# A selective-scan layer and a linear-attention layer in one kernel: the recurrence re-laid as 32 channels by 4 states on the partitions

## The chip, the cores and the metric

The kernel runs on one core of a Trainium2 chip. The metric is the device time of one execution in microseconds (us); less is better. The core has five instruction queues that run side by side, each strictly in its written order: PE (matrix products; PEld is its loading of weights), DVE (vector work, the only engine used here that scans), ACT (functions of one input), POOL (vector work without access to PSUM) and SP, which issues the transfers.

## The reference, cut to what matters

`x` has shape (4, 512, 64, 64): four batches, 512 channels, 4096 positions. Two residual layers follow each other, each fed by a group norm. All data is f32.

```python
# layer 0, on tokens (L = 4096) in four chunks of 128 channels
xn = layer_norm(group_norm(x));  chunk -> 128 channels
xi, z = split(xn_chunk @ in_proj_w.T)            # 256 + 256
xc = silu(causal_conv(xi, 4 taps) + conv_b)      # 256 channels
dt, B, C = split(xc @ x_proj_w.T, 8, 16, 16)
dt = softplus(dt @ dt_proj_w.T + dt_proj_b);  A = -exp(A_log)
h[t] = exp(dt[t] * A) * h[t-1] + dt[t] * xc[t] * B[t]     # 256 channels x 16 states
y[t] = sum over states of h[t] * C[t]
y = (y + xc * D) * silu(z);  chunk_out = y @ out_proj_w.T + skip * xn_chunk
x1 = x + layer_norm(all chunks) @ proj_w.T + proj_b
# layer 1, attention without softmax, 8 heads of 64, on g = group_norm(x1)
q, k = relu(g @ w_q.T + b_q), relu(g @ w_k.T + b_k);  v = g @ w_v.T + b_v
kq = k^T q per head, summed over tokens;  attn = (v @ kq) / (column sums of kq)
out = x1 + attn @ w_out.T + b_out
```

## The kernel before

The positions are cut into 8 tiles of T = 512 for each batch. The unit of work is a **step**: one chunk (c = 0 to 3) of one tile (t) of one batch (b); there are 4 x 8 x 4 = 128 steps. Channels lie on the 128 partitions, so the 256 inner channels are two **halves** (index e), and time runs along the free dimension.

A step has these parts, and the names are those that the profile prints:

- `front` prepares a step while the one before it runs. PE computes `pc` (convolution and input projection folded, 4 matmuls a half) and `pz` (1 a half); ACT takes them out of PSUM (L332, L338; the **front evacuations**), applies silu to both (L297, with a table load before and after). PE computes `pd` (dt, B and C); ACT copies `dtr` and `parts` (L351, L355); L358 on DVE and L362 to L364 on POOL split C into three bf16 parts; the B rows go to DRAM (`b_rows`, L353). PE computes `pt`; five ACT instructions (L374, L375, L377) and then L381, L382 (DVE) and the logarithm L385 form the softplus. The **dt tail** on POOL ends it: `lw` (L387), `dt` (L388), `dtx` = dt * xc (L389), three instructions on 128 x 1024.
- `recurrence` goes through the 16 states. For each: `bx` = dtx * B on POOL (L403; B broadcast over the partitions by a transfer, `b_all`, L398, two states each); `c_all` on PE (L405, C broadcast over the partitions by a bf16 matmul, in the one buffer of the pool `ps_c`); for each half the decay `dA` = exp(A * dt) on ACT (L411, two PSUM buffers) and the scan `h` on DVE (L412), whose last column POOL keeps in `st` (L416); the product `ch` = h * c_all on DVE (L418); and on PE `y` += identity x `ch` (L423), which sums the states in PSUM, one bank a half.
- `gated` closes the step before, within the first state of the new one: the **D-add** on DVE (L431, one a half, reads `y`), the **gate product** on POOL (L434), `po` on PE (L437), and the **ym update** on DVE (L438).

A f32 matmul stands in the trace as two `MATMUL` **pieces**; so the 4096 `y` matmuls are 8192 there.

Three generators are interleaved with the recurrence by `behind()`, called 16 times a step: the next step's `front`; `late` (the next tile's normalisation with L208, L220 to L241; for the last tile the layer norm of `ym`, L223, and the projection `pp` into the residual, L267 to L276); and `rest` (statistics of the next batch and attention of the one before). Attention goes twice over the tiles: first `pq` (L466), the bias add (L472), relu (L475) and `pk` into `kq` (L480, L488); then, with the weights folded into `m3`, the output product `pr` (L546) of the normalised `x1` (L208) with the residual add (L552). It runs within the steps of the next batch, so in batches 1 to 3, and for the last batch after all steps.

All is written for a scheduler that takes these instructions by priority and its own estimates of time and writes out the five queues, and the semaphores; so the order in a queue may differ from that of the text. Every buffer is one of a named pool; a transfer that fills it waits on SP until its last reader is done. The lines of the recurrence that the prediction follows:

```python
c_all = ps_c.tile([P, T], F32, tag="c", name=f"c_all_{nm}_{s}")          # ps_c: bufs=1
nc.tensor.matmul(c_all, sel[:, s : s + 1].to_broadcast([NP, P]), f["parts"], start=True, stop=True)
...
nc.vector.tensor_tensor(ch, h, bc(c_all, NH), ALU.mult)
if s == 0:
    before()                                                             # gated() of the step before
for e in range(NH):
    nc.tensor.matmul(ys[e], ident, ch[:, e, :], start=(s == 0), stop=(s == NST - 1))
behind()
```

Of the kernel before, what the change touches and what calls it, by code (L numbers as in the profile page):

```python
# [14 lines left out]
P = 128  # L15
# [9 lines left out]
def kernel(  # L25
# [33 lines left out]
    NB = 2  # L59
# [16 lines left out]
    def load(src, name):  # L76
        xt = wk.tile([P, NC, T], F32, tag="x", name=name, bufs=4)
        nc.sync.dma_start(xt, src)
        return xt
# [21 lines left out]
    sel = const.tile([NP, NST], BF16, tag="sel", name="sel")  # L101
    for i in range(3):
        r = slice(i * LANE, (i + 1) * LANE)
        nc.vector.tensor_copy(sel[r, :], ident[r, i * LANE : i * LANE + NST])
# [20 lines left out]
    w_x = wk.tile([P, DI], F32, tag="bx", name="w_x", bufs=2)  # L125
    nc.scalar.dma_start(w_x, in_w[:, 0:DI])
    conv_bc = wk.tile([P, NTAP, DI], F32, tag="ch", name="conv_bc", bufs=2)
# [29 lines left out]
    bqk = const.tile([P, 2 * C], F32, tag="bqk", name="bqk")  # L157
    nc.scalar.dma_start(bqk, b_qkv[0 : 2 * C].partition_broadcast(P))
    bv = column(b_qkv[2 * C : 3 * C], NC, "bv")
    bo = column(b_out, NC, "bo")  # L160


    nc.scalar.activation(a_sb, a_sb, AF.Exp)
    nc.vector.tensor_scalar(a_sb, a_sb, -1.0, None, ALU.mult)
# [16 lines left out]
    def stats_end(stats, name):  # L181
# [20 lines left out]
        nc.vector.scalar_tensor_tensor(off, gm, -1.0, gr, ALU.mult, ALU.mult)  # L202
        return gr, off

    def group_norm(dst, xt, norm):
        gr, off = norm
# [39 lines left out]
    def normed(xn, prev, b, t, norm):  # L246

        xt = load_x(b, t, "f")
# [5 lines left out]
        body = xn[:, :, NTAP - 1 : NTAP - 1 + T]  # L254
        group_norm(body, xt, norm)
# [52 lines left out]
    def front_tiles(nm):  # L308
        return {
            n: wk.tile([rows_, *shape], dt_, tag=n, name=f"{n}_{nm}")  # L310
            for n, rows_, shape, dt_ in (
                ("xz", P, (2, NH, T), F32),
                ("dt", P, (NH, T), F32),
                ("dtx", P, (NH, T), F32),
# [4 lines left out]
    def front(f, xn, c, nm):  # L319

        xz, dt, dtx, parts = (f[n] for n in ("xz", "dt", "dtx", "parts"))
# [35 lines left out]
        rest = w[0:NP, 0, :]  # L357
        nc.vector.tensor_tensor(rest, pd[0:NP, :], parts, ALU.subtract)  # L358
        yield
        mid = wk.tile([NP, T], BF16, tag="mid", name=f"mid_{nm}", bufs=1)  # L360
        r1, r2 = slice(LANE, 2 * LANE), slice(2 * LANE, 3 * LANE)
        nc.gpsimd.tensor_copy(parts[r1, :], rest[r1, :])  # L362
        nc.gpsimd.tensor_copy(mid[r2, :], rest[r2, :])
        nc.gpsimd.tensor_tensor(parts[r2, :], rest[r2, :], mid[r2, :], ALU.subtract)  # L364
# [24 lines left out]
        nc.gpsimd.tensor_tensor(dtx, dt, xc, ALU.mult)  # L389
        yield  # L390

    def recurrence(f, st, c, first, nm, before, behind):


        b_all = []
        for s in range(0, NST, NB):
            got = wk.tile([P, NB, T], F32, tag="b_all", name=f"b_all_{nm}_{s}", bufs=4)
            nc.sync.dma_start(got, f["b_rows"][s : s + NB, :].partition_broadcast(P))  # L398
            b_all.append(got)
        ys = []  # L400
        for s in range(NST):
            bx = wk.tile([P, NH, T], F32, tag="bx", name=f"bx_{nm}_{s}", bufs=2)
            nc.gpsimd.tensor_tensor(bx, f["dtx"], bc(b_all[s // NB][:, s % NB, :], NH), ALU.mult)  # L403
            c_all = ps_c.tile([P, T], F32, tag="c", name=f"c_all_{nm}_{s}")
            nc.tensor.matmul(  # L405
                c_all, sel[:, s : s + 1].to_broadcast([NP, P]), f["parts"], start=True, stop=True
            )
            h = wk.tile([P, NH, T], F32, tag="h", name=f"h_{nm}_{s}", bufs=2)
            for e in range(NH):
                dA = ps_d.tile([P, T], F32, tag="dA", name=f"dA_{nm}_{s}_{e}")  # L410
                nc.scalar.activation(dA, f["dt"][:, e, :], AF.Exp, scale=a_sb[:, e, s : s + 1])  # L411
                nc.vector.tensor_tensor_scan(  # L412
# [9 lines left out]
            for e in range(NH):  # L422
                nc.tensor.matmul(ys[e], ident, ch[:, e, :], start=(s == 0), stop=(s == NST - 1))  # L423
# [276 lines left out]
```

## Time and profile before

| what | value |
|---|---|
| median of 3 runs (lowest to highest) | 11519.98 us (11518.61 to 11539.81) |
| the profiled execution: its time, its span | 11542.73 us, 11541.0 us |
| busy: PE, DVE, POOL, ACT | 81%, 75%, 57%, 45% of the span |
| DVE busy, in us | 8695.3 |
| mean granted clock of PE | 0.928 |
| 185 to 2866 us (32 steps, batch 0) | 83.8 us a step |
| 2866 to 5649 us (32 steps, batch 1) | 87.0 us a step |
| 5649 to 8414 us (32 steps, batch 2) | 86.4 us a step |
| 8414 to 11009 us (31 steps, batch 3) | 83.7 us a step |
| 11009 to 11541 us (after the last gate product) | PE busy 439 of 532 us |
| moved by transfers | 793.56 MB, 19.7% of the 16 DMA engines' time |
| `b_all`: 1024 transfers of 512 KB, issue to landing | 3.6 us |
| loads and stores of 1024 KB tiles, issue to landing | 3.8 to 6.8 us |

A row of the costliest groups reads: line, engine, operation, output<-inputs, sizes, count | busy us, mean ns of one | the engine's idle time before these, and what ended most of it. Busy time is a union: pieces of matmuls overlap, so their busy time by count is less than the mean of one. The steps are cut at the starts of the 128 gate products (L434), the first at 185.1 us, the last at 11008.9. A waiting row reads: who waited <- for whom: us in total, times, longest. Shares are averages over the whole span; a step's time comes from which queue holds up which within it.

### The profile page before, as it was taken

Reading aid. Unit: us, or ns where it says so; the run is one execution under the profiler, and the core shown is the slowest. Engines: PE = TensorE matmul, PEld = TensorE weight load, DVE = VectorE, ACT = ScalarE, POOL = GpSimd, SP = SyncE. Lnnn points to the kernel's source line nnn. Section 1 sums busy time; section 2 is a strip of 40 time slices with the busy share of each in tenths; the row PEclk is TensorE's granted clock in tenths of the full one; section 3 lists DMA queues with packets and bytes.
Section 4 is the critical chain, followed back from the end, with each engine's and each line's share of the span. In section 5 each row is a group of like instructions: output and inputs, shape, how many; then the busy total and the mean of one; then the engine's idle time right before and its main releaser. Section 6 shows DMA issues by size and latency. Waiting matters only on the chain.

```text
span 11541.0 us, 69580 instructions
## 1 busy us (share of the span) xinstructions
PE 9309.0 (81%) x20832; PEld 3741.0 (32%) x20832; DVE 8695.3 (75%) x8177; ACT 5230.3 (45%) x7460; POOL 6599.1 (57%) x5045
## 2 busy tenths in 40 slices
PE   5777777777788888888788888888888888888878
PEld 2222222222333333333333333333333333333333
DVE  6777777787777777787877777777777887878831
ACT  3444444444444544444444444444444545444421
POOL 4666666566565565565566565566565665656600
PEclk8999898988899998999999999999999999999999
DMA  4111111121111111122311111122211111112201
GB/s 138 61 63 54 60 61 64 59 89 63 47 69 64 63 64 66 59 84 83 101 62 66 54 64 64 62 72 85 84 66 64 66 70 63 67 65 84 89 24 66
DMA packets 244443, 793.56 MB, mean 69 GB/s; under 512 B 27224, under 2 KB 27744, under 8 KB 231776
## 3 DMA queue, kind: packets, MB, share of 16 engines
q1 hardware_dynamic: 237184, 784.42, 19.7%
q10 hardware_dynamic: 6880, 4.70, 0.1%
q8 instruction: 163, 2.67, 0.1%
q14 instruction: 216, 1.77, 0.0%
HBM read 717.73 MB, written 71.30 MB: 68 GB/s over the span
## 4 chain that ended last, share of the span: by engine, by line
PE 36%; DVE 34%; POOL 15%; ACT 8%; issue 7%; DMA 0%; DVEq 0%; ACTq 0%; POOLq 0%; SPq 0%
DVE h L412 20%; PE y L423 14%; DVE ch L418 10%; PE pc L326 8%; POOL bx L403 7%; PE pq L466 4%; PE po L437 3%; POOL dt L388 2%; POOL dtx L389 2%; POOL lw L387 2%; POOL xz L434 2%; PE pz L334 2%; PE c_all L405 2%; ACT L297 1%; ACT xz L297 1%
## 5 line engine op out<-in xcount | busy, mean ns | idle before, releaser
L423 PE MATMUL y<-ch,ident 128*128 128x512 f32 x8192 | 4492.7, 676 | 1754.9 <-DVE ch L418 1753.3
L412 DVE TENSOR_TENSOR_SCAN h<-dA,st,bx 128x512 f32<-128x512 f32 x3584 | 4414.9, 1269 | 569.8 <-ACT dA L411 201.2
L403 POOL TENSOR_TENSOR bx<-dtx,b_all 128x1024 f32<-128x1024 f32 x2048 | 4819.0, 2353 | 0.7 <-POOL st L416 0.6
L411 ACT ACTIVATE dA<-dt,a_sb 128x512 f32<-128x512 f32 x4096 | 2815.2, 691 | 3793.0 <-DVE h L412 3778.0
L418 DVE TENSOR_TENSOR ch<-h,c_all 128x1024 f32<-128x1024 f32 x2048 | 2470.4, 1206 | 954.4 <-PE c_all L405 945.6
L423 PEld LDWEIGHTS y<-ch,ident 128*128 128x128 f32 x8192 | 1559.6, 205 | 4322.9 <-DVE ch L418 3063.7
L416 POOL COPY st<-h 128x2 f32<-128x2 f32 x2048 | 380.2, 186 | 4055.2 <-DVE h L412 4007.6
L466 PE MATMUL pq<-w_qk,xa 128*128 128x512 f32 x2048 | 982.6, 608 | 8.6 <-ACT xa L208 4.0
L326 PE MATMUL pc<-xn,w_cv 128*128 128x512 f32 x2048 | 971.8, 599 | 4.2 <-ACT xn L241 4.2
L405 PE MATMUL c_all<-parts,sel 96*128 96x512 bf16 x2048 | 825.3, 403 | 0.0
L332 ACT ACTIVATE xz<-pc,cb 128x512 f32<-128x512 f32 x256 | 175.9, 687 | 1411.9 <-PE pc L326 1411.7
L412 DVE TENSOR_TENSOR_SCAN h<-dA,bx 128x512 f32<-128x512 f32 x512 | 599.3, 1208 | 104.5 <-POOL bx L403 49.7
L466 PEld LDWEIGHTS pq<-w_qk,xa 128*128 128x128 f32 x2048 | 394.5, 196 | 470.9 <-issue 420.9
L326 PEld LDWEIGHTS pc<-xn,w_cv 128*128 128x128 f32 x2048 | 394.9, 193 | 465.1 <-issue 448.6
L267 PE MATMUL pp<-ym,w_pr 128*128 128x512 f32 x1024 | 491.4, 604 | 13.5 <-DVE ym L243 13.5
L546 PE MATMUL pr<-gn,m 128*128 128x512 f32 x1024 | 482.6, 602 | 12.9 <-ACT gn L208 9.6
L437 PE MATMUL po<-xz,w_op 128*128 128x512 f32 x512 | 315.3, 746 | 148.8 <-POOL xz L434 148.5
L472 DVE TENSOR_TENSOR qk<-pq,bqk 128x512 f32<-128x512 f32 x256 | 174.3, 681 | 298.8 <-PE pq L466 298.8
L405 PEld LDWEIGHTS <-sel 96*128 96x128 bf16 x2048 | 215.6, 105 | 558.3 <-issue 536.3
L387 POOL TENSOR_TENSOR lw<-lw,dtx 128x1024 f32<-128x1024 f32 x128 | 301.6, 2356 | 135.0 <-ACT lw L385 135.0
L438 DVE SCALAR_TENSOR_TENSOR ym<-xn,sk,po 128x512 f32<-128x512 f32 x128 | 95.7, 747 | 325.1 <-PE po L437 325.1
L346 PE MATMUL pd<-xz,w_xp 128*120 128x512 f32 x512 | 271.9, 654 | 77.0 <-ACT xz L297 77.0
(125 smaller groups left out, 7353.8 us busy)
## 6 DMA issues: line engine op xcount, KB each, us to landing
b_all<-b_rows SPq DMA_DIRECT2D x1024, 512.0 KB, 3.6
xs<-in_x_dram SPq DMA_DIRECT2D x32, 1024.0 KB, 6.3
xf<-in_x_dram SPq DMA_DIRECT2D x32, 1024.0 KB, 6.7
xr<-in_x_dram SPq DMA_DIRECT2D x32, 1024.0 KB, 5.7
x<-xr SPq DMA_DIRECT2D x32, 1024.0 KB, 3.8
xa<-x SPq DMA_DIRECT2D x32, 1024.0 KB, 5.3
xb<-x SPq DMA_DIRECT2D x32, 1024.0 KB, 5.1
out_dram<-xb SPq DMA_DIRECT2D x32, 1024.0 KB, 4.2
```

What stands on the lines that cost most here:

```text
L267: nc.tensor.matmul(pp, w_pr[:, c, o * P : (o + 1) * P], ym[:, c, :], start=(c == 0), stop=(c == NC - 1),)
L326: nc.tensor.matmul(pc, w_cv[:, k, e * P : (e + 1) * P], xn[:, c, k : k + T], start=(k == 0), stop=(k == NTAP - 1),)
L387: nc.gpsimd.tensor_tensor(w, w, q, ALU.subtract)
L403: nc.gpsimd.tensor_tensor(bx, f["dtx"], bc(b_all[s // NB][:, s % NB, :], NH), ALU.mult)
L405: nc.tensor.matmul(c_all, sel[:, s : s + 1].to_broadcast([NP, P]), f["parts"], start=True, stop=True)
L411: nc.scalar.activation(dA, f["dt"][:, e, :], AF.Exp, scale=a_sb[:, e, s : s + 1])
L412: nc.vector.tensor_tensor_scan(h[:, e, :], dA, bx[:, e, :], 0.0 if first else st[:, c, s, e : e + 1], ALU.mult, ALU.add,)
L418: nc.vector.tensor_tensor(ch, h, bc(c_all, NH), ALU.mult)
L423: nc.tensor.matmul(ys[e], ident, ch[:, e, :], start=(s == 0), stop=(s == NST - 1))
L437: nc.tensor.matmul(po, w_op[:, e, :], sz[:, e, :], start=(e == 0), stop=(e == NH - 1))
L466: nc.tensor.matmul(pq, gn[:, c, u * P : (u + 1) * P], w_qk[:, c, j * C : (j + 1) * C], start=(c == 0), stop=(c == NC - 1),)
L546: nc.tensor.matmul(pp, m3[:, m, o * P : (o + 1) * P], gn[:, m, :], start=(m == 0), stop=(m == NC - 1),)
```

## The change

The recurrence is laid out anew. A tile holds 32 channels by 4 states on its 128 partitions (partition = state index k in the group x 32 + channel), so a half of 128 channels is four blocks j, and the 16 states are four groups q. The recurrence goes through 8 groups (half e, group q), each with two **pairs** of blocks; a pair is one `bx`, two `dA`, two scans, one `st` copy and one product, of the same shapes as a state had before. The product is written over `bx` (three buffers, held until `y` has read it). One `c_all` serves a group, and the next group's is written ahead of this group's `y` in the text. `y` is summed by a 128 x 32 matrix `fold` (four stacked identities) into 32 of the 128 partitions. `dt` and `dtx`, one buffer now, go to DRAM (`d_rows`) after the dt tail and come back spread to the new layout (`spread`, eight transfers of 256 KB a half); `b_all` becomes four transfers of 64 KB a group. In attention the q/k bias enters through a bf16 matmul of three parts, relu reads PSUM, the second group norm is folded into `m3` (with an identity for the residual) and `ob`, and outputs leave by quarters of a tile. The input tile of a normalisation is loaded in place.

```diff
+        nc.vector.tensor_copy(
+            sel[r].rearrange("p q k i -> p (q k) i"),
+            ident[r, i * LANE : i * LANE + NST].unsqueeze(2).to_broadcast([LANE, NST, BLK]),
+        )
...
+    fold = const.tile([P, BLK], F32, tag="fold", name="fold")
+    for k in range(KS):
+        r = slice(k * BLK, (k + 1) * BLK)
+        nc.vector.tensor_copy(fold[r, :], ident[r, r])
...
-        xt = load_x(b, t, "f")
+        body = xn[:, :, NTAP - 1 : NTAP - 1 + T]
+        nc.sync.dma_start(body, cols(x, b)[:, :, t * T : (t + 1) * T])
...
-        xz, dt, dtx, parts = (f[n] for n in ("xz", "dt", "dtx", "parts"))
+        xz, parts = f["xz"], f["parts"]
+        both = wk.tile([P, 2, NH, T], F32, tag="dt", name=f"dt_{nm}", bufs=1)
+        dt, dtx = both[:, 0], both[:, 1]
...
         nc.gpsimd.tensor_tensor(dtx, dt, xc, ALU.mult)
-        yield
+
+        f["d_rows"] = []
+        for v in range(2):
+            d_rows = dram.tile([P, NH, T], F32, tag=f"d_rows{v}", name=f"d_rows{v}_{nm}")
+            nc.sync.dma_start(d_rows, both[:, v])
+            f["d_rows"].append(d_rows)
+        yield
+        spread(f, 0, nm)
+        yield
+
+    def spread(f, e, nm):
+        d = wk.tile([P, 2, NJ, T], F32, tag="d_all", name=f"d_all_{nm}_{e}")
+        for v in range(2):
+            src = f["d_rows"][v].rearrange("(j i) e t -> i e j t", i=BLK)[:, e]
+            for k in range(KS):
+                nc.sync.dma_start(d[k * BLK : (k + 1) * BLK, v], src)
+        f["d_all", e] = d
...
+        groups = [(e, q) for e in range(NH) for q in range(NQ)]
+        b_all = {g: b_row(*g) for g in groups[:NQ]}
+        c_all = c_row(*groups[0])
         ys = []
...
+        for n, (e, q) in enumerate(groups):
+            if n == 1:
+                spread(f, 1, nm)
+            if n == NQ - 1:
+                b_all.update({g: b_row(*g) for g in groups[NQ:]})
+            d = f["d_all", e]
+            chs = []
+            for jj in range(JJ):
+                k2 = f"{nm}_{e}_{q}_{jj}"
+                js = slice(jj * 2, jj * 2 + 2)
+                bx = wk.tile([P, 2, T], F32, tag="bx", name=f"bx_{k2}", bufs=3)
+                nc.gpsimd.tensor_tensor(bx, d[:, 1, js, :], bc(b_all[e, q], 2), ALU.mult)
+                h = wk.tile([P, 2, T], F32, tag="h", name=f"h_{k2}", bufs=2)
+                for i in range(2):
+                    j = jj * 2 + i
+                    dA = ps_d.tile([P, T], F32, tag="dA", name=f"dA_{k2}_{i}")
+                    nc.scalar.activation(dA, d[:, 0, j, :], AF.Exp, scale=a_t[:, e, j, q : q + 1])
+                    nc.vector.tensor_tensor_scan(
+                        h[:, i, :], dA, bx[:, i, :],
+                        0.0 if first else st[:, c, e, q, j : j + 1], ALU.mult, ALU.add,
+                    )
+                nc.gpsimd.tensor_copy(st[:, c, e, q, js], h[:, :, T - 1])
+
+                nc.vector.tensor_tensor(bx, h, bc(c_all, 2), ALU.mult)
+                chs.append(bx)
+                if n == 0 and jj == 0:
+                    before()
+                if jj < JJ - 1:
+                    behind()
+            if n + 1 < len(groups):
+                c_all = c_row(*groups[n + 1])
+            if q == 0:
+                ys.append(ps_y.tile([P, T], F32, tag="y", name=f"y_{nm}_{e}"))
+            for jj in range(JJ):
+                for i in range(2):
+                    r = slice((jj * 2 + i) * BLK, (jj * 2 + i + 1) * BLK)
+                    nc.tensor.matmul(
+                        ys[e][r, :], fold, chs[jj][:, i, :], start=(q == 0), stop=(q == NQ - 1)
+                    )
             behind()
...
+                    nc.tensor.matmul(
+                        pq, sel[:, 0, 0:1].to_broadcast([NP, P]), bqk[:, j * C : (j + 1) * C],
+                        start=True, stop=False,
+                    )
...
-                    nc.vector.tensor_tensor(
-                        qk[:, j * C : (j + 1) * C], pq, bqk[:, j * C : (j + 1) * C], ALU.add
-                    )
-                nc.scalar.activation(qk, qk, AF.Relu)
+                    nc.scalar.activation(qk[:, j * C : (j + 1) * C], pq, AF.Relu)
...
-            nc.scalar.copy(m3[:, m, :], pm)
+            nc.scalar.activation(m3[:, m, :], pm, AF.Copy, scale=gr[:, m : m + 1])
...
-            gn = wk.tile([P, NC, T], F32, tag="gn", name=f"gn_{b}_{t}", bufs=1)
-            group_norm(gn, res, norm)
...
-                nc.vector.scalar_tensor_tensor(
-                    res[:, o, :], pp, ob[:, o : o + 1], res[:, o, :], ALU.add, ALU.add
-                )
+                res = wk.tile([P, T], F32, tag="res", name=f"res_{b}_{t}_{o}")
+                nc.scalar.activation(res, pp, AF.Identity, bias=ob[:, o : o + 1])
+                nc.sync.dma_start(cols(out, b)[:, o, t * T : (t + 1) * T], res)
                 yield
```

`b_row` issues the four `b_all` transfers of a group, `c_row` the `c_all` matmul with 128 columns of `sel`; `before()` is the `gated` of the step before.

## The prediction

> **What bounds the kernel now.** I read the page first, then the waits of DVE, then one plain step engine by engine in the timeline (a step: one 128-channel chunk of one 512-column tile; 128 of them). The page's chain and costliest groups:
>
> ```profile
> PE 36%; DVE 34%; POOL 15%; ACT 8%; issue 7%; DMA 0%; DVEq 0%; ACTq 0%; POOLq 0%; SPq 0%
> ...
> L423 PE MATMUL y<-ch,ident 128*128 128x512 f32 x8192 | 4492.7, 676 | 1754.9 <-DVE ch L418 1753.3
> L412 DVE TENSOR_TENSOR_SCAN h<-dA,st,bx 128x512 f32<-128x512 f32 x3584 | 4414.9, 1269 | 569.8 <-ACT dA L411 201.2
> ...
> L418 DVE TENSOR_TENSOR ch<-h,c_all 128x1024 f32<-128x1024 f32 x2048 | 2470.4, 1206 | 954.4 <-PE c_all L405 945.6
> ```
>
> No engine is full: the end is set by a loop of scan, product `ch`, sum `y` and `c_all`. The waits of DVE (total, times, longest):
>
> ```profile
> DVE ch L418 <- PE c_all L405: 945.6, 591, 5.7
> DVE ym L438 <- PE po L437: 325.1, 126, 5.8
> DVE qk L472 <- PE pq L466: 298.8, 106, 7.6
> DVE h L412 <- POOL bx L403: 242.9, 164, 12.5
> DVE h L412 <- ACT dA L411: 233.2, 100, 5.6
> ```
>
> The first is what the change can take away: one PSUM buffer for `c_all`, queued on PE behind the `y` of the state before. Next, the timeline of a plain step (start, duration), DVE at its end:
>
> ```profile
> 1335.91 1.20 DVE L418 TENSOR_TENSOR ch<-h,c_all 128x1024 f32<-128x1024 f32 x1
> 1337.23 2.46 DVE L412 TENSOR_TENSOR_SCAN h<-dA,st,bx 128x512 f32<-128x512 f32 x2
> 1339.61 1.19 DVE L418 TENSOR_TENSOR ch<-h,c_all 128x1024 f32<-128x1024 f32 x1
> ...
> 1344.63 2.46 DVE L412 TENSOR_TENSOR_SCAN h<-dA,st,bx 128x512 f32<-128x512 f32 x2
> 1347.01 0.72 DVE L431 SCALAR_TENSOR_TENSOR xz<-xz,dpar,y 128x512 f32<-128x512 f32 x1
> 1347.65 1.21 DVE L418 TENSOR_TENSOR ch<-h,c_all 128x1024 f32<-128x1024 f32 x1
> ```
>
> Undisturbed, a pair of scans and its product take 3.70 us (1335.91 to 1339.61). And at the handover the next step's scans stand ahead of the last step's L431, so its chain (L431, POOL L434, PE L437, DVE L438) is covered. POOL and PE of the same step:
>
> ```profile
> 1309.69 2.34 POOL L403 TENSOR_TENSOR bx<-dtx,b_all 128x1024 f32<-128x1024 f32 x1
> 1311.99 2.34 POOL L388 TENSOR_TENSOR dt<-dt,lw 128x1024 f32<-128x1024 f32 x1
> 1314.41 2.35 POOL L389 TENSOR_TENSOR dtx<-dt,xz 128x1024 f32<-128x1024 f32 x1
> ```
> ```profile
> 1322.84 3.78 PE L423 MATMUL y<-ch,ident 128*128 128x512 f32 x4 [4.28 <-DVE ch L418]
> ...
> 1333.46 1.98 PE L423 MATMUL y<-ch,ident 128*128 128x512 f32 x4 [1.31 <-DVE ch L418]
> ```
>
> A `bx` is ready ahead while POOL does the dt tail (L387 to L389, 7.05 us). A f32 matmul is two pieces of 0.43 us each (1.98 for four, with 0.25 after the last); at the low clock four take 3.78. This step took 82.1 us (from one L434 to the next); by batches a step takes 83.8, 87.0, 86.4 and 83.7 us, after 185 and before a tail of 532.
>
> **What the change leaves as it is.** Scans (4096), products (2048), `bx` (2048), exponentials (4096) and `y` pieces (8192) keep count and size, 16 pairs a step. DVE loses the qk add (174.3 busy, 298.8 waited) and the last residual add (94.8 and 134.4). `c_all` halves to 1024 and in the built order stands ahead of the later half of a group's `y`: I price its wait at 0 to 1 us a step, take 0. Folding of constants, `m3` and the input load in place cost nothing: small or off the path; without their cover, 0.2 us each.
>
> **What it moves: the built order.** In before, ACT does the exponentials of four states of the new step ahead of the next front's first evacuation; in after, of one pair. In 123 of 127 handovers DVE has D-add and `ym` update ahead of the new step's first scan; in 120 of 128 steps POOL has the whole dt tail between the last `st` copy of channel half 0 and the first `bx` of half 1. Each is now a serial stretch. I walk a plain step, 0 being the end of the last product:
>
> 1. Handover. `y`, four pieces at the mean busy 0.548: 2.2. D-add 0.73: 3.0. Gate product on POOL 2.34: 5.4. `po` at mean busy 0.616 by four, 2.46: 7.9. `ym` update 0.75: 8.7. Only now the first scans, 2.46: 11.2. Queued behind these is the whole recurrence. The second pair waits for more: its exponentials stand on ACT behind four evacuations, the last of which needs the 20 pieces of `pc` and `pz` that PE has after `po`: 7.9 + 8.6 + 0.25 + 0.58 (L338) + 0.69 (exponential) = 18.0. DVE worked 3.9 of it.
> 2. Six scans and three products: 6 x 1.23 + 3 x 1.20 = 11.0.
> 3. To the last scan of half 0: eight scans 9.84, four products 4.8, L358 0.67, and two waits of 1.1 for exponentials, which ACT has behind silu with its table loads (1.28 + 1.91 + 1.28) and behind five dt activations (four by 0.68, one 1.07): 17.4. Before has the same two waits' causes; its wait of 4.46 in this step is that for silu.
> 4. Dt tail. L382, product, L382 and the logarithm: 0.68 + 1.20 + 0.68 + 0.60 = 3.2. Then POOL: three by 2.35 and half 1's first `bx` 2.35, with hand-offs 9.5: 12.7. DVE has 3.3 of work in it (the two L382, the product, a D-add) and idles 9.4.
> 5. Half 1's eight pairs at 3.70: 29.6. POOL needs 2.35 + 0.18 for a pair and stays ahead; a `bx` buffer, now held until its `y` is done, comes back some 4.9 us before it is needed again less 4.8 for `y`, copy and `bx`: it just fits, and at the low clock it would miss by 1.8.
>
> Sum 88.7, against 82.1. Where c=0, the `ym` mean (8 pieces, then 2.29 of L223) also stands before the first scan, +3.7, and 22 pieces of projection before the last residual, +4.8: 97.2. Where c=1, the next tile's normalisation (4 x 0.80 on ACT, L223 on DVE) stands in stretch 3: +5.2, less 0.8 for fewer pieces: 93.1. Mean 91.9. With attention, the order puts on average 1.9 us of `pq` ahead of the last evacuation in the c=2 and c=3 steps (+1.0 a step), and the `kq` adds are 0.7 a step: 93.6.
>
> **Bounds.** Start: written rows 3.8 (row of x<-xr) and two spreads of 1 MB at 5.3 (row of xa<-x), +15. Tail: PE is busy 439 of 532; -93 if all its idle went, +14 for 64 bf16 biases at 0.22; I take 0. Low clock: PE idles some 3 us before `po`; by the two `y` rows it adds 0 to 1.8 to the last `y` and as much to `po` and `pc`, so 0 to 3.6 a step; the mean over that step's sixteen `y` groups is 2.53, 0.3 above what I used, and for `po` and `pc` I take half of their 1.8: 1.2 in all. A 32-column `y` piece is in no row: its bounds are 0.13 (the bf16 `c_all`, 0.38 less its end) and 0.9 (a quarter of the low-clock 3.78 less its end); nearest in type and length is the 128-column f32 piece, taken unchanged. A change of it counts only in the handover, by four: -1.2 to +1.9 a step.
>
> By the Trainium skill (TensorE: Matmul & The Clock Gate, Part 3) matmuls on distinct column groups run together, 2.38 times faster for three: 1 us less a step. Against it stands TensorEngine Tiling, Key Properties: a change of tiling mode drains the array, and here `c_all` stands between `y` groups; by the 0.25 above, two such drains on the path make 0.5 us more a step. No row shows either.
>
> DMA: front and recurrence of a step issue 51 transfers instead of 9, at 0.32 to 0.42 each (SP's rows in the timeline): 20 us of SP. Moved data is 7 MB a step against 4. The new chain starts when the dt tail ends (stretch 4, 10.4 in): rows written 3.8, a `b_all` that waits for two `bx` (4.7), eight spreads, 3.2 to issue, 10.6 to read: 22 us, with some 40 until the next step needs them. Hidden; uncovered, each us costs 128. SP waits behind `b_rows` for ACT, with half 1's `b_all` queued behind: 14 us ahead of their use.
>
> **Sum.** 185 + 15 + 31 x 91.9 + 96 x 93.6 + 532 = 12567; clock, 127 x 1.2 = 152: 12719. The profiled execution took 11542.7, 0.2% above the median, so 12700.
>
> **Rivals.** Faster: the handover and dt-tail gaps (14.1 and 9.4) are covered, as the scans already stood behind POOL and ACT before, and the removed waits decide: 945.6 + 298.8 + 174.3 + 134.4 + 94.8 = 1648 less, 9890; with the gaps half covered 12700 - 127 x 11.8 = 11200. It decides once the gaps together fall below some 14 us a step. For it: `c_all` is DVE's largest wait. Against: queues run in order, and both gaps consist of row durations. 0.09. Slower still: the spreads, 256 KB each, take 6 us one after another instead of 3.6 for a 512 KB broadcast (b_all's row): 48 instead of 11, past the 40, some 12 us a step: 14200. 0.07. Column tiles share no time, or drain (the change doesn't do what it says): PE is not the bound, 12700 to 12800; within the forecast. Break-even by chance: 0.02.
>
> **How the numbers follow.** Forecast 0.82, alone 12200 to 13300 (clock and hidden waits both ways). The range for 8 in 10 reaches a little to both rivals: 12050 to 13400. What a measurement tells from no change is about 0.2%. Faster 0.09, same 0.02, slower 0.89.
>
> **What would show it.** DVE busy about 8430, PE's `c_all` wait under 150; new at the top: scans waiting for ACT's exponentials (9 a step, about 1100) and for POOL's `bx` (about 800), `ym` for `po` (about 600), D-add for `y` (about 290). Plain steps of 88 to 91. Wrong if the scans wait for `d_all` loads, or if the sums of these four stay under 1500.

## The result and the profile after

The changed kernel takes 13006.6 us (median of four runs, 13005.5 to 13009.5) against 11519.3 for the kernel before: 1.129 times as long, 95% interval 1.127 to 1.131. The forecast was 12700, range 12050 to 13400. The profiled execution has a span of 13003.7 us. From its page, the busy times, TensorE's granted clock in tenths and two of the three costliest groups:

```profile
PE 8839.4 (68%) x20192; PEld 2528.6 (19%) x20192; DVE 8484.0 (65%) x7826; ACT 5208.4 (40%) x7588; POOL 6629.6 (51%) x5045
...
PEclk7666666666677777777777777777777777777879
...
L480 DVE TENSOR_TENSOR_SCAN h<-dA,st,bx 128x512 f32<-128x512 f32 x3584 | 4438.5, 1270 | 1564.5 <-ACT dA L479 830.1
L499 PE MATMUL y<-bx,fold 128*32 128x512 f32 x8192 | 3362.2, 918 | 1902.2 <-DVE bx L486 1892.3
```

A scan costs what it did (1270 ns); in front of the scans DVE now idles 1564.5 us instead of 569.8. The waits of DVE (total, times, longest) say for what:

```profile
DVE h L480 <- ACT dA L479: 915.3, 324, 15.1
DVE ym L516 <- PE po L515: 751.7, 124, 6.3
DVE h L480 <- POOL bx L474: 749.3, 132, 28.3
DVE kq L567 <- PE pk L559: 593.0, 103, 13.4
DVE xz L509 <- PE y L499: 411.9, 223, 7.1
...
DVE bx L486 <- PE c_all L456: 30.6, 15, 4.6
```

The `c_all` wait of 945.6 is gone, as forecast, and the four waits of the handover and the dt tail stand in its place; between them is one the forecast did not have, `kq` for `pk`. The timeline of a plain step without attention (start, duration, in brackets the idle time before it and its releaser), from the end of the last product at 1503.0 to the next step's handover:

```profile
1505.05 0.75 DVE L509 SCALAR_TENSOR_TENSOR xz<-xz,dpar,y 128x512 f32<-128x512 f32 x1 [2.02 <-PE y L499]
1505.88 2.34 POOL L512 TENSOR_TENSOR xz<-xz 128x1024 f32<-128x1024 f32 x1 [3.86 <-DVE xz L509]
1508.27 3.68 PE L515 MATMUL po<-xz,w_op 128*128 128x512 f32 x4 [2.94 <-POOL xz L512]
1511.99 0.75 DVE L516 SCALAR_TENSOR_TENSOR ym<-xn,sk,po 128x512 f32<-128x512 f32 x1 [6.19 <-PE po L515]
1512.65 2.45 DVE L480 TENSOR_TENSOR_SCAN h<-dA,st,bx 128x512 f32<-128x512 f32 x2
...
1521.05 1.30 ACT L479 ACTIVATE dA<-d_all,a_t 128x512 f32<-128x512 f32 x2
1521.85 1.28 DVE L480 TENSOR_TENSOR_SCAN h<-dA,st,bx 128x512 f32<-128x512 f32 x1 [6.75 <-ACT dA L479]
...
1553.12 2.35 POOL L417 TENSOR_TENSOR lw<-lw,dt 128x1024 f32<-128x1024 f32 x1 [2.77 <-ACT lw L415]
1555.54 2.34 POOL L418 TENSOR_TENSOR dt<-dt,lw 128x1024 f32<-128x1024 f32 x1
1557.96 2.34 POOL L419 TENSOR_TENSOR dt<-dt,xz 128x1024 f32<-128x1024 f32 x1
1560.25 4.64 POOL L474 TENSOR_TENSOR bx<-d_all,b_all 128x1024 f32<-128x1024 f32 x2
1562.63 2.46 DVE L480 TENSOR_TENSOR_SCAN h<-dA,st,bx 128x512 f32<-128x512 f32 x2 [7.51 <-POOL bx L474]
```

This is the walk of the forecast, row by row: y, D-add, gate product, `po`, ym update, two scans, the wait for exponentials; later the three POOL products and a `bx`. DVE's idle time at the handover is 2.02 + 6.19 + 6.75 = 15.0 us (forecast 14.1) and at the dt tail 7.5 plus 2.0 ahead of a D-add (forecast 9.4). The next gate product starts at 1594.5, a step of 88.7 us.

### The profile page after: what moved, and what is told of

It reads as the page before. It is cut to its first block, busy times and chain, and to the rows that moved or that the text cites. A ratio compares the mean times of both kernels' runs of the same rounds, so it can differ in the third digit from the quotient of the medians.

```text
span 13003.7 us, 77842 instructions
## 1 busy us (share of the span) xinstructions
PE 8839.4 (68%) x20192; PEld 2528.6 (19%) x20192; DVE 8484.0 (65%) x7826; ACT 5208.4 (40%) x7588; POOL 6629.6 (51%) x5045
## 3 DMA queue, kind: packets, MB, share of 16 engines
q14 instruction: 292, 2.38, 0.1%
## 5 line engine op out<-in xcount | busy, mean ns | idle before, releaser
L474 POOL TENSOR_TENSOR bx<-d_all,b_all 128x1024 f32<-128x1024 f32 x2048 | 4792.1, 2349 | 1525.9 <-PE y L499 1297.4
L480 DVE TENSOR_TENSOR_SCAN h<-dA,st,bx 128x512 f32<-128x512 f32 x3584 | 4438.5, 1270 | 1564.5 <-ACT dA L479 830.1
L499 PE MATMUL y<-bx,fold 128*32 128x512 f32 x8192 | 3362.2, 918 | 1902.2 <-DVE bx L486 1892.3
L479 ACT ACTIVATE dA<-d_all,a_t 128x512 f32<-128x512 f32 x4096 | 2793.3, 690 | 4143.4 <-DVE h L480 4118.3
L486 DVE TENSOR_TENSOR bx<-h,c_all 128x1024 f32<-128x1024 f32 x2048 | 2469.9, 1206 | 91.2 <-PE c_all L456 30.6
L456 PE MATMUL c_all<-parts,sel 96*128 96x512 bf16 x1024 | 544.9, 532 | 1475.6 <-DVE bx L486 1470.7
L499 PEld LDWEIGHTS y<-bx,fold 128*32 128x32 f32 x8192 | 355.5, 130 | 3942.6 <-DVE bx L486 3148.7
L480 DVE TENSOR_TENSOR_SCAN h<-dA,bx 128x512 f32<-128x512 f32 x512 | 597.5, 1207 | 181.4 <-POOL bx L474 94.8
L515 PE MATMUL po<-xz,w_op 128*128 128x512 f32 x512 | 449.8, 1029 | 338.1 <-POOL xz L512 338.1
L516 DVE SCALAR_TENSOR_TENSOR ym<-xn,sk,po 128x512 f32<-128x512 f32 x128 | 95.6, 747 | 751.7 <-PE po L515 751.7
L512 POOL TENSOR_TENSOR xz<-xz 128x1024 f32<-128x1024 f32 x128 | 299.3, 2338 | 507.1 <-DVE xz L509 471.4
L417 POOL TENSOR_TENSOR lw<-lw,dt 128x1024 f32<-128x1024 f32 x128 | 301.0, 2352 | 419.2 <-ACT lw L415 419.2
L632 PE MATMUL pr<-xb,m 128*128 128x512 f32 x1024 | 502.7, 636 | 5.7 <-ACT lw L415 2.3
L567 DVE TENSOR_TENSOR kq<-pk,kq 128x512 f32<-128x512 f32 x124 | 85.2, 687 | 593.0 <-PE pk L559 593.0
```

The costliest lines, as they stand in the source:

```text
L456: nc.tensor.matmul(c_all, sel[:, q, :], f["parts"], start=True, stop=True)
L474: nc.gpsimd.tensor_tensor(bx, d[:, 1, js, :], bc(b_all[e, q], 2), ALU.mult)
L479: nc.scalar.activation(dA, d[:, 0, j, :], AF.Exp, scale=a_t[:, e, j, q : q + 1])
L480: nc.vector.tensor_tensor_scan(h[:, i, :], dA, bx[:, i, :], 0.0 if first else st[:, c, e, q, j : j + 1], ALU.mult, ALU.add,)
L486: nc.vector.tensor_tensor(bx, h, bc(c_all, 2), ALU.mult)
L499: nc.tensor.matmul(ys[e][r, :], fold, chs[jj][:, i, :], start=(q == 0), stop=(q == NQ - 1))
```

## The experiments

Each was timed beside the kernel before on the same chip; that took 11497 to 11532 us by the chip, so a difference of some 35 us between two rows is read from the ratios or not at all. "Steps" are the mean times from one gate product to the next in batches 0 to 3, from the profiled run; attention runs beside batches 1 to 3.

| kernel | us | times before, 95% interval | clock | steps, us |
|---|---|---|---|---|
| before | 11519.3 | | 0.928 | 83.8, 87.0, 86.4, 83.7 |
| changed | 13006.6 | 1.1287 (1.1268 to 1.1307) | 0.738 | 93.5, 98.6, 98.8, 96.8 |
| e1 dt tail moved | 12648.1 | 1.0971 (1.0954 to 1.0987) | 0.746 | 89.4, 96.3, 96.3, 94.8 |
| e2 handover moved | 12223.2 | 1.0603 (1.0585 to 1.0621) | 0.762 | 87.2, 92.9, 92.6, 90.2 |
| e3 both | 11452.6 | 0.9935 (0.9916 to 0.9954) | 0.772 | 81.9, 86.6, 86.4, 83.8 |
| e4 kq add moved | 13011.7 | 1.1286 (1.1269 to 1.1303) | 0.736 | 93.6, 98.8, 98.8, 96.7 |
| e5 attention in half 1 | 12905.6 | 1.1222 (1.1203 to 1.1241) | 0.742 | 93.4, 97.4, 97.4, 96.2 |
| e6 both, and e5 | 11618.9 | 1.0102 (1.0087 to 1.0117) | 0.764 | 81.8, 88.0, 87.8, 86.3 |
| e7 before, in the changed order | 13258.0 | 1.1529 (1.1512 to 1.1546) | 0.893 | 95.4, 100.8, 100.5, 98.2 |
| e8 before, attention part alone | 11353.6 | 0.9874 (0.9859 to 0.9888) | 0.940 | 83.8, 85.2, 84.7, 82.9 |
| e9 full-array y | 12885.1 | 1.1185 (1.1168 to 1.1201) | 0.894 | 94.8, 96.5, 96.7, 95.8 |
| e10 both, full-array y | 11668.9 | 1.0131 (1.0116 to 1.0146) | 0.904 | 83.1, 88.7, 88.5, 85.5 |
| e11 one column group | 12957.5 | 1.1246 (1.1227 to 1.1265) | 0.819 | 94.8, 98.0, 98.2, 96.1 |
| e12 double loads | 13293.1 | 1.1540 (1.1522 to 1.1557) | 0.724 | 97.2, 100.3, 100.3, 98.8 |

An order is forced with one helper, a dependency that only the build sees and that adds no wait:

```diff
+    ORDER = mybir.DependencyInfo(mybir.DependencyClass.NoSync, mybir.DependencyReason.DATA)
+    def later(i, first):
+        tc.add_manual_dep(i.ins, first.ins.name, ORDER, reason="order")
+    held = {}
```

**e1, the dt tail behind the first bx of half 1.**

```diff
-        nc.gpsimd.tensor_tensor(w, w, q, ALU.subtract)
-        nc.gpsimd.tensor_tensor(dt, dt, w, ALU.add)
-        nc.gpsimd.tensor_tensor(dtx, dt, xc, ALU.mult)
+        held["tail"] = [
+            nc.gpsimd.tensor_tensor(w, w, q, ALU.subtract),
+            nc.gpsimd.tensor_tensor(dt, dt, w, ALU.add),
+            nc.gpsimd.tensor_tensor(dtx, dt, xc, ALU.mult),
+        ]
...
+                if e == 1 and held.get("tail"):
+                    later(held["tail"].pop(0), made)   # made: this pair's bx
```

> The changed kernel, with only the order of POOL's queue forced: the three operations of the dt tail stand each behind one bx of channel half 1 (behind the second, third and fourth), where the build had all three ahead of the first. DVE's order at the handover is kept (ym update ahead of the first scan in 124 handovers). Theory (the order makes the stall): the dt tail's idle stretch, 9.4 us a step by the walk and 749.3 us of scan waits for bx in the trace, goes for the most part: -5 to -7 us a step, 12100 to 12400 us against 13006.6; scan waits for bx under 250. Rival (the loads of d_all are what is late): the tail ends some 7 us later, so the written rows and spreads come later, and the first bx of the next step waits: 13000 or more.

Measured: 12648.1, 359 less, half of what was expected. DVE's waits of this kernel:

```profile
DVE h L491 <- ACT dA L490: 984.2, 348, 15.6
...
DVE h L491 <- POOL bx L483: 327.3, 153, 28.4
```

The wait for `bx` fell by 422, to 327.3 where under 250 was expected, and some of it came back as waiting for exponentials. The rival, late loads, would have made it slower; it did not.

**e2, the handover behind the new step's first scans.**

```diff
+        if "scan" in held:
+            later(dadd, held["scan"])          # last D-add behind the first scans
...
+                if n == 0 and jj == 1 and "ym" in held:
+                    later(held.pop("ym"), held["scan"])
+                if n == 1 and jj == JJ - 1:
+                    for i in held.pop("evac", []):
+                        later(i, held["exp"])  # first xz<-pc behind four pairs' exponentials
...
```

The same helper keeps the dt tail ahead of half 1's first `bx` in every step.

> The changed kernel, with only the handover's order forced: the last D-add stands behind the new step's first two scans, the ym update behind the second pair's scans, and ACT's first front evacuation behind the exponentials of four pairs; the dt tail stays ahead of half 1's first bx. Theory (the order makes the stall): ym waiting for po (751.7 us in the changed kernel), D-add for y (411.9) and about half of the scans' wait for exponentials (915.3) go, -10 to -13 us a step: 11400 to 11750 us. Rival (TensorE's low granted clock of 0.738 is the cause): the clock stays as low and the products and evacuations are only late elsewhere: above 12700.

Measured: 12223.2, 783 less, more than half of what was expected. What was late next:

```profile
DVE h L497 <- POOL bx L487: 1395.0, 400, 26.3
DVE h L497 <- ACT dA L494: 859.1, 212, 9.8
...
DVE bx L503 <- PE c_all L469: 304.6, 145, 4.3
...
DVE ym L540 <- PE po L539: 131.2, 112, 6.3
```

`po` is covered (751.7 to 131.2), but the scans now run into `bx`: 400 waits instead of 132. The `c_all` wait that the new placing had removed is partly back (30.6 to 304.6); that TensorE has the front's pieces beside the recurrence again fits this. The clock did not explain the stall: it rose by only 0.024 while the time fell 6%.

**e3, both orders forced** (the edits of e1 and e2 together).

> The changed kernel with both orders forced, that of the dt tail and that of the handover. Theory: both gaps go, and with the removed c_all and q/k waits the step comes to 16 pairs of 3.70 plus 10 to 16 us, 70 to 76 us: 9900 to 10700 us in all, below the kernel before (11519), and TensorE's granted clock rises above 0.80 as it idles less. Rival (the layout itself costs, by its loads, column tiles or the pairs' buffers): not below 11500.

Measured: 11452.6, 1554 less than the changed kernel and 0.65% below the kernel before. The two edits bring 1142 one by one and 1554 together: each gap had partly hidden behind the other. So the built order of two places was worth more than the whole slowdown of 1487. The time is below the rival's limit of 11500, by 48, but the expectation's upper end, 10700, was too low by 750, and the clock, 0.772, did not reach 0.80. Left over are waits for exponentials (one of 6.5 us in a plain step behind silu and its table loads), `bx` and `c_all`:

```profile
DVE h L497 <- ACT dA L494: 907.4, 221, 9.8
DVE h L497 <- POOL bx L487: 696.1, 374, 26.7
DVE bx L503 <- PE c_all L469: 328.1, 139, 5.6
```

Where no attention runs, a plain step takes 79.2 us, 2.7 less than the same step of before.

**e7, the reverse: the kernel before in the changed kernel's order.**

```diff
+        if "bx" in held:
+            later(held.pop("bx"), dtx_made)      # latest bx behind the whole dt tail
...
+            if e == NH - 1 and "exp" in held:
+                later(held.pop("exp"), evac)     # state 1's exponential behind all four evacuations
...
+            for e in range(NH):
+                later(held[f"scan{e}"], ym_made) # state 0's scans behind the ym update
```

> The kernel before, with only the order of the changed kernel forced on it: the ym update ahead of the new step's first scans, all four front evacuations ahead of the second state's exponentials, and the dt tail ahead of the bx of state 8. Theory (the order alone makes the stalls, whatever the layout): it loses what the walk prices as the two gaps, 14.1 and 9.4 us a step, less what the c_all and bx waits of before already stand there for; 10 to 18 us a step, 12800 to 13800 us, more than the whole change cost. Rival (the new layout, its loads and its pairs make the stalls): under 12000.

Measured: 13258.0, 15.3% above the kernel before beside it: 13.8 us a step. DVE's waits:

```profile
DVE h L427 <- POOL bx L414: 937.0, 129, 12.5
DVE ch L435 <- PE c_all L418: 800.7, 573, 4.3
DVE h L427 <- ACT dA L424: 778.3, 174, 10.5
DVE ym L455 <- PE po L454: 718.7, 128, 6.3
```

In before these were 242.9, 945.6, 233.2 and 325.1: three rise by 1633 together, `c_all` falls by 145. With none of the new layout, no DRAM copies and no column tiles, the order alone costs more than the change did. The clock here is 0.893, so the stalls are not those of a slow TensorE either. The trace has the forced order in every handover and dt tail; the changed kernel has it in 122 or 123 of 127 handovers and 120 of 128 tails, so this run is slightly the stricter. With e3 it settles the main cause.

**e8, the attention part of the change alone, on the kernel before** (q/k offset as a bf16 product with the relu reading PSUM, and the last product folded with the residual; the diff is the attention hunks of the change).

> The kernel before with the attention part of the change alone: the q/k offset as a product on TensorE and the relu read from PSUM by quarters, the folded last product with the residual in m3, and ACT instead of DVE for the last evacuation. Theory (the terms of the forecast for DVE: 298.8 waited and 174.3 busy for the q/k add, 134.4 and 94.8 for the last residual, of which the scans get the part that is not taken over by the kq add's wait): 200 to 500 us less, 11000 to 11320. Rival (these waits stood in for late work on TensorE and come back as waits for pk): within 1%, 11400 to 11600.

Measured: 11353.6, a gain of 1.26%, 143 us, below the expected range. It is the fastest version run. DVE waits for the q/k product no more; three other waits grew, for exponentials from 233.2 to 311.9, for `c_all` from 945.6 and for `pk` from 121.4:

```profile
DVE ch L434 <- PE c_all L421: 1031.5, 593, 6.0
...
DVE kq L505 <- PE pk L497: 307.0, 55, 8.5
```

**e4, the kq add back behind the second pair's scans.** It asks whether the 593.0 us of `kq` for `pk` are what the attention steps cost beyond the forecast.

```diff
+                    held["kq"] = nc.vector.tensor_tensor(kq, pk, kq, ALU.add)
...
+                            later(i, held["scan"])   # i: the add issued a pair ago
```

> The changed kernel, with only the kq add of the attention moved back on DVE's queue, behind the scans of the second pair after it is issued; handover and dt tail as built. Theory (the term that the forecast lacked): the add stood ahead of scans while pk was not yet there, 593 us of waiting in 103 waits; -4 us a step over 95 steps, 12550 to 12750 us, and the mean step of batches 1 and 2 falls from 98.7 to 94 to 95 us. Rival (the wait only stands in for work that is late anyway, the scans behind it having waited for bx and exponentials): less than 0.7% is gained, 12920 or more.

Measured: 13011.7, unchanged; the theory fell. The wait itself left, and two others took it over:

```profile
DVE h L487 <- ACT dA L486: 1095.1, 343, 15.1
DVE h L487 <- POOL bx L481: 904.3, 139, 26.8
...
DVE kq L581 <- PE pk L573: 262.3, 31, 8.5
```

The 331 us that it lost are the 335 that the scans' two waits gained (915.3 to 1095.1, 749.3 to 904.3). DVE had stood at a place where the next work was late as well, as the rival has it: a wait names who came last, not what it would give back.

**e5, attention beside half 1 only.**

```diff
-        def behind():
+        def behind(e):
             next(nxt, None)
-            for queue in (late, rest):
+            for queue in (late,) + (rest,) * (3 if e else 0):
...
```

Averaged start times of the changed kernel, counted from the gate product, show where attention's TensorE pieces (22 to 26 us a step at c=2 and c=3) are felt; batch 0 has none, the second figure is that of batches 1 and 2:

| step | last front evacuation ends | dt tail starts | step |
|---|---|---|---|
| c=0 | 18.7, 19.5 | 52.5, 54.0 | 96.9, 99.4 |
| c=1 | 33.9, 35.9 | 58.6, 59.9 | 100.0, 102.1 |
| c=2 | 15.3, 22.4 | 47.1, 55.1 | 88.4, 97.2 |
| c=3 | 15.4, 20.5 | 47.2, 56.4 | 88.5, 96.0 |

> The changed kernel, with the attention's pieces issued only beside channel half 1 (three at a call) instead of beside both halves, so that TensorE's attention products stand less between po, the front's pieces and the dt tail's inputs. Theory (attention products delay the front's last evacuation by 5 to 7 us and the dt tail by 8 us in the c=2 and c=3 steps, and that is the missing 3.5 us a step): the mean step of batches 1 and 2 falls from 98.7 to 94.5 to 96.5 us, 12650 to 12850 us in all against 13006.6. Rival (the attention steps are longer by their DVE and ACT work, wherever it stands): within 0.5% of the changed kernel, 12940 or more.

Measured: 12905.6, only 101 less (75 by the ratios); neither theory nor rival holds. At c=3 it went as the theory has it: dt tail at 46.7, step 91.6. At c=2 the pieces, now ending late in half 1, stand ahead of `po`: it starts 9.5 us after the gate product instead of 2.4, and the step stays at 97.1. These are means of unlike steps: of the eight c=2 steps of a batch, three have no attention piece ahead of `po` and take 88.6, and in the other five `po` starts 2.9 to 28.9 us after the gate product and the step takes 91 to 111. c=1 became longer (103.9), c=0 shorter (96.8). The position of attention's pieces sets who waits; most of their cost only moved.

**e6, e3 with e5's placing.**

> Both orders forced, as in the run that gave 11452.6, with the attention's pieces beside half 1 only. Theory (the same delay is left in that kernel, whose batches 1 and 2 have 86.6 us a step against 81.9 in batch 0): 2 to 3 us a step less, 11150 to 11300 us. Rival (with the gaps closed DVE has no room left in half 1 for the added work): 11400 or more.

Measured: 11618.9, some 1.5% slower than e3, in the rival's range. Its reason, no room left in half 1, fits; no run tried it by itself.

**e9 and e10, y over the full array.** Each piece takes 128 columns, its own 32 filled:

```diff
-    fold = const.tile([P, BLK], F32, tag="fold", name="fold")
+    fold = const.tile([P, 2 * P - BLK], F32, tag="fold", name="fold")   # zeros, the fold in columns 96 to 127
...
-                        ys[e][r, :], fold, chs[jj][:, i, :], start=(q == 0), stop=(q == NQ - 1)
+                        ys[e], fold[:, P - (j + 1) * BLK : 2 * P - (j + 1) * BLK], chs[jj][:, i, :],
+                        start=(q == 0 and j == 0), stop=(q == NQ - 1 and j == NJ - 1),
```

> The changed kernel with y summed over all 128 columns of the array instead of column tiles of 32: each piece takes a 128x128 matrix that holds the fold in its own 32 columns and zeros elsewhere, and all four pieces accumulate in the whole bank. Count of pieces, handover and dt tail as built. Theory (the column tiles, not TensorE's idling, keep the granted clock at 0.738; the kernel before with the changed order idled about as much and had 0.893): the clock rises to 0.85 or more, a po takes 2.5 us instead of 3.7, a pair's... four y pieces take 2.0 us instead of 1.05 at full clock and 1.92 at low; the two balance: within 1.5% of the changed kernel, 12820 to 13200 us. Rival (idle time sets the clock): it stays at 0.72 to 0.78, four pieces take 3.6 to 3.8 us, and the time rises above 13250.

> Both orders forced, as in the run that gave 11452.6, and y over the full array as in the run beside this one. Theory (clock kept low by column tiles): clock above 0.85, po and the front's pieces at full speed against y at 2.0 us for four: 11200 to 11550 us. Rival (idle time sets the clock): the clock stays near 0.77 and the y sums, which hold the bx buffers, make the scans wait for bx: above 11700.

Measured: 12885.1 (0.9% less than the changed kernel) and 11668.9 (1.9% more than e3, where less or the same was expected). From e9's page:

```profile
PE 9395.7 (73%) x20192; PEld 3773.9 (29%) x20192; DVE 8480.5 (66%) x7827; ACT 5223.3 (41%) x7588; POOL 6659.6 (52%) x5045
...
PEclk8888888888898899998899888999898999998989
...
L517 PE MATMUL po<-xz,w_op 128*128 128x512 f32 x512 | 353.0, 827 | 338.3 <-POOL xz L514 338.3
```

The clock goes from 0.738 to 0.894, as the theory has it, and the mean `po` piece from 1029 to 827 ns; at handover and dt tail the order is that of the changed kernel in nearly every step. So the column tiles are why the clock was low. But it doesn't show what the theory adds, that TensorE's idling has no part in this: the two busy shares of 73%, of e3 and e9, can't be compared, since a piece takes longer at the low clock. Multiplied by the clock granted while busy (0.80 and 0.90), e3 has 6682 us of work at full clock and e9 8415: four y pieces take 1.05 us in one and 1.88 to 1.98 in the other.

The traces tell more. In each the granted clock is either half or full, and it changes only at multiples of 3.41 us. Cut into stretches of this length, they show which clock came after a stretch, by how much of it PE was busy (the ends of matmuls are modelled):

| kernel | times at half clock, mean us | full, busy under 40%: low next | half, busy under 80%: full next | half, busy 80% or more: full next |
|---|---|---|---|---|
| before | 334, 5.0 | 180 of 180 | 0 of 126 | 333 of 362 |
| changed | 490, 13.9 | 390 of 390 | 0 of 1442 | 489 of 552 |
| e3 | 325, 16.1 | 178 of 178 | 0 of 1098 | 324 of 433 |
| e9 | 457, 6.0 | 384 of 384 | 1 of 311 | 455 of 488 |
| e11 (below) | 555, 8.5 | 356 of 356 | 0 of 758 | 554 of 620 |

The borders are the same with and without column tiles. The clock falls about as often in e9 as in the changed kernel (457 and 490 times), but comes back sooner: 61% of e9's half-clock stretches are busy for 80% or more, 28% of the changed kernel's, whose y pieces are over sooner. So idle time does set the clock, stretch by stretch, and the column tiles act mainly through the idle time they leave. A smaller effect of their own is not excluded: of full-clock stretches busy for half or more, 65 of 1339 were followed by the low clock in the changed kernel, 32 of 2403 in e9.

What the tiles are worth hangs on the order: with the gaps open they cost 0.9%; with the gaps closed they bring 1.9%. That they let `bx` buffers go sooner fits (scans waited 887.4 us for `bx` in e10, 696.1 in e3), but the layer norm's wait for its mean grew by 143 too, and no run separates these.

**e11, groups 1 and 2 of y in one column group.**

```diff
-                    r = slice((jj * 2 + i) * BLK, (jj * 2 + i + 1) * BLK)
+                    g = jj * 2 + i if q in (0, NQ - 1) else 0
+                    r = slice(g * BLK, (g + 1) * BLK)
```

> The changed kernel, where the y pieces of the state groups 1 and 2 all go into the first 32 columns of the array (the sums of these groups are thereby left out of the other channels); groups 0 and 3 keep their four column tiles. It measures what distinct column tiles share. Theory (pieces to distinct columns run side by side in pairs): four pieces of groups 1 and 2 take 1.98 us at full clock and 3.6 to 3.8 at the low one, those of groups 0 and 3 stay at 1.05 and 1.92; the time rises by less than 1%, 13000 to 13140. Rival (a 32-column piece is simply shorter): all stay at 1.05 and 1.92.

Measured: 12957.5, a little under the expected range. A stretch of its timeline on PE at full clock (the `c_all` of 0.39 shows that; at the low clock it takes 0.61):

```profile
1525.52 0.39 PE L456 MATMUL c_all<-parts,sel 96*128 96x512 bf16 x1 [3.20 <-DVE bx L486]
1525.84 1.90 PE L500 MATMUL y<-bx,fold 128*32 128x512 f32 x4
1529.00 1.05 PE L500 MATMUL y<-bx,fold 128*32 128x512 f32 x4 [1.25 <-DVE bx L486]
1531.45 1.05 PE L500 MATMUL y<-bx,fold 128*32 128x512 f32 x4 [1.40 <-DVE bx L486]
```

A row of four is two f32 products of two pieces each. In the first row all go to one column group, in the next two each product has its own: 1.90 against 1.05. Distinct column tiles run side by side, two at a time (the trace has them start 0.01 us apart, the next two 0.45 later), 1.8 times as fast. Four at a time was not tried. The clock, with half of the pieces no longer side by side though still 32 columns wide, is 0.819, between 0.738 and 0.894: how long PE is busy counts, as in the table above.

**e12, twice the transfers.**

```diff
+                spare = dram.tile([BLK, NJ, T], F32, tag="spare", name=f"sp_{nm}_{e}_{v}_{k}", bufs=8)
+                nc.sync.dma_start(spare, src)
```

> The changed kernel with each of the sixteen spreads of d_rows followed by a copy of the same 256 KB to a spare place in DRAM: 16 transfers and 4 MB more a step on the same queue, nothing reads them. Theory (the loads of d_all have some 18 us of cover and are not what the slowdown consists of): within 0.7%, 12920 to 13100 us. Rival (loads late or contention between the queues): above 13250.

Measured: 13293.1, 2.2% more than the changed kernel, so the number is the rival's. Its mechanism is not: a spread still lands in 6.6 us (7.8 in the changed kernel), and POOL's waits of `bx` for transfers are 176 us in all against 153. What changed is the built order: in 123 of 127 steps no exponential of the new step is ahead of the front's evacuations any more, where the changed kernel has one pair's in 122. In a plain step the first scans then wait

```profile
1489.01 3.63 DVE L482 TENSOR_TENSOR_SCAN h<-dA,st,bx 128x512 f32<-128x512 f32 x3 [9.96 <-ACT dA L481]
```

and the rest of the handover is as before. So the run did not isolate contention, which stays open; it shows that transfers that nothing reads can move the built order of another engine's queue. That the DRAM copies are also why the changed kernel was built with its order fits this, but was not tried by itself.

## Why the prediction held, and which step was off

- **Cause.** Right. The serial stretches at the handover and the dt tail are the slowdown: undone they give back 1554 us (e3), put on the kernel before they cost 1761 (e7). The four waits named as new sum to 2828, above the 1500 set as the limit; exponentials 915.3, `bx` 749.3 and `po` 751.7 are near the 1100, 800 and 600 given, D-add 411.9 against 290.
- **Plain step.** Forecast 88.7 and 1.2 for the clock; measured 88.4 to 88.5 in batch 0. `po` took 3.68 instead of 2.46, half 1 was a little shorter.
- **c=0 and c=1.** Mis-sized in opposite directions: with the clock 98.4 and 94.3 forecast, 96.9 and 100.0 measured. Batch 0's mean, 93.1 forecast and 93.5 measured, came out right partly by that.
- **Attention, the term that failed.** "The order puts on average 1.9 us of `pq` ahead of the last evacuation ... and the `kq` adds are 0.7 a step": 1.7 in all, no wait priced. The steps of batches 1 to 3 are 5.1, 5.3 and 3.3 us above batch 0's. Against the forecast's 94.8 (93.6 and the clock) that is 3.8, 4.0 and 2.0 more, over 32, 32 and 31 steps 312 us. That is the gap of 285 between 12719 and the span: batch 0 and the start add 12 and 5, the tail takes off 41. The evacuation was delayed by 5 to 7 us at c=2 and c=3 and the dt tail by 8 to 9. The profile of before held a warning: its own steps grow by 3.2 us from batch 0 to batch 1. e4 shows that the `kq` wait was only a sign; e5 gets a quarter to a third back by moving the pieces. How the rest divides between TensorE and ACT stays open.
- **Removed waits.** `c_all` went as forecast. Of the 702 us for the q/k add and the last residual, e8 shows 143 on the path.
- **Clock.** Its reason, PE idling ahead of `po`, holds: every full-clock stretch busy under 40% was followed by the low clock. What the prediction left out is that shorter y pieces then keep the clock low; it let their length count in the handover alone, and no mean clock of 0.738 follows from its terms. The 1.2 us itself can't be checked by one row: `po` alone took 1.2 more than in the walk, yet the plain step stayed below the sum without the allowance.
- **y pieces.** Taken unchanged, though four run in 1.05 us at full clock. At the low clock they took 1.92, and the D-add waited 2.02 against 2.2 forecast. The Trainium skill (TensorE: Matmul & The Clock Gate, Part 3), whose 2.38 for three tiles was set beside the sum, points the right way: e11 has 1.90 over 1.05, 1.8 for two column groups. The drain set against it, 0.25 us a change of tiling, is smaller here: `y` starts 0.32 us after a `c_all` at full clock, and 0.22 or 0.23 in e9, where there are no tiles; 0.1 us a change.
- **Loads.** Hidden as forecast: on the changed kernel's POOL, `bx` waited 129.2 us in all for `b_all` and 23.4 for `d_all`. The rival that had them late did not come about; its price was also off, as 22 + 37 us against a cover of 40 is 19 a step, not 12.
- **The faster rival** did not come about either: with both gaps closed the changed kernel gains 0.65%, not the 3 to 14% priced for it. And the attention part alone gains 1.26% (e8), so this is not the layout's. Beside e8, e3's steps are 1.9 us shorter in batch 0, where no attention runs, and 1.4, 1.7 and 0.9 longer in the others: in sum e3 is 0.6% slower. So the new recurrence layout, its order mended, gains without attention beside it and loses with it; why was not tried, nor the layout without the attention part.

## What to carry to other kernels

When a change adds latency ahead of a loop, read the built order of each queue before counting operations: here the order of two places was worth 12 to 15%, and the new recurrence layout, its order mended, no gain over the attention part alone. A wait in the table is not a saving until an experiment removes it; moving the `kq` add gave nothing, as the work behind it was late as well. Take what a background task costs now from the steps with and without it, not from its pieces.

## What the runs showed of the hardware

Four f32 pieces, two each to two column groups, take 1.05 us, to one group 1.90, both at full clock. The mean granted clock was 0.738 with all y pieces side by side in column tiles, 0.819 with half of them, 0.894 with none, TensorE being busy 68, 71 and 73% of the span. The Trainium skill (TensorE: Matmul & The Clock Gate, Part 1) lets the clock follow how busy TensorE has been, and the stretches of 3.41 us agree: in all fourteen traces, 4335 of 4335 full-clock stretches busy under 40% were followed by half the clock, and 1 of 12302 half-clock stretches busy under 80% by the full one. The mean busy share over the span doesn't give it: e3 and e9, both 73%, have 0.772 and 0.894.
